# A recurrence on one core: inputs of both batch halves in one instruction, the state in unused ends of buffers, and a sixth place for the layer's blocks

## The chip, the cores and the metric

The kernel runs on one core of a Trainium2 chip. The metric is the device time of one execution in microseconds (us). Three runs of the kernel before took 1663.87, 1656.67 and 1659.29 us, a median of 1659.29. A further execution, taken by the hardware profiler, gives the profile; it took 1664.5 us, of which the profile's span covers 1661.4.

The engines have these names: TensorE (PE: matrix products and transposes), VectorE (DVE), ScalarE (ACT), GpSimd (POOL) and SyncE (SP), which here issues transfers (DMA). SBUF is the on-chip memory, PSUM the memory into which TensorE writes. Shapes are given as partitions x elements.

## What is computed

The input x has 16 images of 56 x 56 positions with 128 channels. Cut to what matters:

```python
x = x + window_attention(group_norm(x))          # 7x7 windows, shifted, 4 heads
t = to_tokens(x)                                 # [16, 3136, 128]
t = t + linear_attention(layer_norm(t))          # cumulative, elu + 1
n = layer_norm(t)
Wx = batch_norm(n @ W.T)                         # over all 16 * 3136 tokens; gamma, beta
y = 0                                            # [16, 128]
for i in range(3136):
    y = sigmoid(Wx[:, i] + y @ V.T)
    t[:, i] = t[:, i] + y
return from_tokens(t)
```

The change concerns the last loop, the recurrence, and the residual that is added to it. W, V and the batch norm's factors are small and stay on the chip; x3 below is t before the recurrence, xs is n @ W.T before the batch norm.

## The kernel before

**Until 1497 us: the two attention stages.** Image by image, a planner (`Plan`) lays out the steps of windows, linear attention and projection on the engines by given costs, and the order it finds is written out. At the end of each image, x3 goes to a buffer in DRAM (`x_d` in the profile), and so does xs (`xs_d`, written from `staged`). For the last image, whose last part never leaves the chip, GpSimd copies from `staged` (L356). The batch norm's factor `bsc` and shift `bsh` come from statistics over all images (`bst` holds those of the parts); VectorE computes them at 1499 to 1502 us, L1684 to L1703, with one step on GpSimd (L1695).

**From 1497 us: the recurrence.** 3136 steps in a row would be too long. Each image's steps are cut into 32 segments (`SEG`) of 98 steps (`CH`), and all 16 x 32 segments run side by side. A segment's start is the end of the one before, which isn't known yet. So twelve steps of warm-up (`WARM`) are run ahead: the last twelve of each segment, started from nothing, give a start `y0` for the segment after it. At the end, `yend` (the true ends) is compared with `y0` (L1895 to L1907), and only where they differ is the loop repeated; with these inputs it isn't.

A step is done in two halves of the batch, `g` = 0 and 1, 8 images each, 8 x 32 = 256 columns. Steps are taken in pairs: 6 pairs of warm-up, 49 pairs of the main loop. The order is written out by hand, and the engines follow it through semaphores:

- **VectorE, `inputs` (L1773):** multiplies xs by `bsc` and writes it into a PSUM buffer `z_buf`. There are six of these, three for each half, each with a pair's two steps (128 x 512 elements, one PSUM bank). It is done two pairs ahead, between the two steps of a pair, one instruction per half. Blocks of xs hold 7 steps (`KB`); a pair whose two steps lie in two blocks needs two instructions of 256 elements per half. That happens at 7 of the 49 pairs.
- **TensorE (L1785):** adds V times the state to `z_buf`, 128 x 256 for each half-step, as two passes in the profile. **ScalarE (L1788)** takes the sigmoid with `bsh` as bias and writes the new state `y` to SBUF.
- **TensorE (L1822):** transposes the state of the step before, two transposes of 128 x 128 in each half-step, into a PSUM tile `pot` of which there are two.
- **VectorE, `plus_layer` (L1831):** after both halves adds the tile to the x3 block in place (128 x 512).
- **SyncE:** after every 7 steps the finished x3 block is stored (L1837, 1792 KB), and a later block is loaded (`load_x3`, L366, 1792 KB) into the place of the block before, which waits until that block's store has landed. xs blocks come the same way (`load_xs`, L344, 1680 KB).

There are 14 blocks of each kind. xs has a ring of five places. x3 has five too: `x3_ring` begins with three buffers that earlier stages used (`xw_buf` twice, `oT_buf`; in the profile these names), and two tiles of its own (`x_ring` in the profile). The loads that can be issued before the loop are issued at 1490 to 1499 us. Block m of x3 takes the place of block m - 5, and its load is issued behind the store of block m - 4. The last x3 block is stored in two pieces, the last one of 768 KB.

The state of four steps is kept in the pool `ryo` (two buffers of a pair each, `y` or `y_a` in the profile), y0 and yend have tiles of their own, and y0 is set to zero by GpSimd (L1721). Six matmuls of zeros (L1734) prepare the PSUM buffers once.

Of the kernel before, what the change touches and what calls it, by code (L numbers as in the profile page):

```python
# [10 lines left out]
F32 = mybir.dt.float32  # L11
AF = mybir.ActivationFunctionType
ALU = mybir.AluOpType
# [11 lines left out]
KB = 7  # L25
# [209 lines left out]
def tile_conv_attn_hybrid(  # L235
# [19 lines left out]
    nc = tc.nc  # L255
    B, H, W, C = x.shape
    P = 128
# [17 lines left out]
    NU = H // WS  # L275
# [10 lines left out]
    NQ = B // 4  # L286
# [10 lines left out]
    xw_bufs = [hold.tile([P, NU, 512], F32, name=f"xw_buf{i}") for i in range(2)]  # L297
    oT_buf0 = hold.tile([P, NU, 512], F32, name="oT_buf0")
# [59 lines left out]
    def flat(to):  # L358

        dims = " ".join("abc"[: len(to.shape) - 1])  # L360
        return to.rearrange(f"p {dims} -> p ({dims})")
# [60 lines left out]
    bst = const.tile([P, B * NS, 6], F32, name="bst")  # L422
# [7 lines left out]
    with ExitStack() as s1:  # L430
# [141 lines left out]
        s = issued = plan.step("SP", 0.1, -1.0, lambda: None, takes=[weights], lag=19.0)  # L572
# [987 lines left out]
        for b in range(B):  # L1560
# [12 lines left out]
            for g in range(NG):  # L1573
# [3 lines left out]
                up, xs, pj = token_group(  # L1577
                    b,
                    g,
                    b * NG + g,  # L1580
                    t,
                    loaded[g] if b else turns[g],
                    [rows[u] for u in need],
                    oT_buf,
                    xt_bs[g],
# [107 lines left out]
        bsc = const.tile([P, 1], F32, name="bsc")  # L1693
# [16 lines left out]
    SEG = NCH  # L1710
    GB = B // 2
# [3 lines left out]
    )  # L1715
    with ExitStack() as s2:
        rin = s2.enter_context(tc.tile_pool(name="rin", bufs=1))
        ryo = s2.enter_context(tc.tile_pool(name="ryo", bufs=2))
        y0 = rin.tile([P, B, SEG], F32, name="y0")
        yend = rin.tile([P, B, SEG], F32, name="yend")  # L1720
        nc.gpsimd.memset(y0, 0.0)  # L1721


# [1 line left out]
        psum = bass.MemoryType.PSUM  # L1725
        ps_s = s2.enter_context(tc.tile_pool(name="ps_s", bufs=1, space=psum))
        ps_o = s2.enter_context(tc.tile_pool(name="ps_o", bufs=2, space=psum))
        z_bufs = [
            ps_s.tile([P, 2, GB, SEG], F32, name=f"z_buf{i}") for i in range(6)
        ]  # L1730
        BF16 = mybir.dt.bfloat16
        zeros = y0.rearrange("p b s -> p (b s)").bitcast(BF16)[:, 0 : B * SEG]
        for i in (0, 3, 1, 4, 2, 5):
            nc.tensor.matmul(  # L1734
                z_bufs[i].rearrange("p k b s -> p (k b s)"),
                ident.bitcast(BF16)[:, 0:P],
                zeros,
                start=True,
                stop=True,
                skip_group_check=True,  # L1740
            )
# [7 lines left out]
        xs_ring += [xt for xt in xt_bufs if all(xt is not to for to in used)]  # L1749
        xs_ring += [rin.tile([P, G * NG, C], F32, name=f"xs_ring{i}") for i in range(2)]  # L1750

        x3_ring = [ahead["x3"][m] for m in range(3)]
        x3_ring += [rin.tile([P, NQ, KB, C], F32, name=f"x3_ring{i}") for i in range(2)]
        NX, N3 = len(xs_ring), len(x3_ring)

        def xs_of(m):
            to = ahead["xs"][m] if m >= NJ - 2 else xs_ring[m % NX]
            return to.rearrange("p n c -> p (n c)").rearrange(
                "p (b k n) -> p b k n", b=B, k=KB
            )  # L1760
# [5 lines left out]
        def inputs(pair):  # L1766

            j, ns, slot, _ = pair
            (m, k), (m2, k2) = divmod(j, KB), divmod(j + 1, KB)
            parts = [(m, k, 0, 2)] if m == m2 else [(m, k, 0, 1), (m2, k2, 1, 1)]  # L1770
            for g in range(2):
                for m, k, i, n in parts:
                    nc.vector.tensor_scalar(  # L1773
                        z_bufs[3 * g + slot][:, i : i + n, :, 0:ns],
                        xs_of(m)[:, GB * g : GB * (g + 1), k : k + n, 0:ns].rearrange(
                            "p b k s -> p k b s"
                        ),
                        bsc,
                        None,
                        ALU.mult,  # L1780
                    )

        def step(z, y_prev, y):
            if y_prev is not None:
# [5 lines left out]
        def segments(n, prev):  # L1790


            warm = prev is None


            pairs = []
            if warm:
                prev = [None, None]
                for j in range(CH - WARM, CH, 2):
                    pairs.append((j, SEG - 1, len(pairs) % 3, True))  # L1800
            for j in range(0, CH, 2):
                pairs.append((j, SEG, len(pairs) % 3, False))

            def load_inputs(m):
                if m not in ahead["xs"] or n != "a" and m < NJ - 2:
                    load_xs(xs_ring[m % NX], m, 0, B - 1)
                    last_xs(xs_ring[m % NX], m)

            def load_layer(m):
                first = NQ - 1 if n == "a" and m in ahead["x3"] else 0  # L1810
                load_x3(x3_ring[m % N3], m, first, NQ)

            blocks = {}

            def turned_half(at, h):

                m, k = at
                y = blocks[at]
                if h == 0:
                    blocks["po"] = ps_o.tile([P, NQ, C], F32, tag="o", name=f"pot_{n}{m}_{k}")  # L1820
                for q in range(NQ // 2 * h, NQ // 2 * (h + 1)):
                    nc.tensor.transpose(  # L1822
                        blocks["po"][:, q, :],
                        y[:, 4 * q : 4 * (q + 1), :].rearrange("p b s -> p (b s)"),
                        ident,
                    )

            def plus_layer(at):
                m, k = at
                o = x3_of(m)  # L1830
                nc.vector.tensor_tensor(  # L1831
                    o[:, :, k, :], blocks["po"], o[:, :, k, :], ALU.add
                )
                cuts = (KB // 2 + 1, KB) if m == NJ - 1 else (KB,)
                if k + 1 in cuts:
                    k0 = 0 if k + 1 == cuts[0] else cuts[0]
                    nc.sync.dma_start(  # L1837
                        out_q[:, :, KB * m + k0 : KB * m + k + 1, :], o[:, :, k0 : k + 1]
                    )

                    if k == KB - 1 and m and m - 1 + N3 < NJ:
                        load_layer(m - 1 + N3)

            for m in range(3):
                load_layer(m)
            for m in range(NX):
                load_inputs(m)
                if m >= 3:
                    load_layer(m)
            assert N3 == NX  # L1850
            inputs(pairs[0])
            inputs(pairs[1])
            last = None
            for p, (j, ns, slot, warming) in enumerate(pairs):
                y = ryo.tile([P, 2, B, SEG], F32, tag="y", name=f"y_{n}_{p}")
                if not warming:
                    for i in range(2):
                        blocks[divmod(j + i, KB)] = y[:, i]
                for i in range(2):
                    for g in range(2):  # L1860
                        gb = slice(GB * g, GB * (g + 1))
                        if not warming:
                            to = y[:, i, gb, :]
                        elif j + i == CH - 1:
                            to = y0[:, gb, 1:SEG]
                        else:
                            to = y[:, i, gb, 0:ns]
                        z = z_bufs[3 * g + slot][:, i, :, 0:ns]
                        if not warming and j + i == 0:
                            prev[g] = y0[:, gb, :]  # L1870
                        step(z, prev[g], to)
                        prev[g] = to
                        if last is not None:
                            turned_half(last, g)
                    if last is not None:
                        plus_layer(last)
                    if not warming:
                        last = divmod(j + i, KB)
                    if i == 0 and p + 2 < len(pairs):
                        inputs(pairs[p + 2])  # L1880
                        j2, _, _, warming2 = pairs[p + 2]
                        m2 = j2 // KB
                        if not warming2 and (j2 + 2) // KB > m2 and m2 + NX < NJ:
                            load_inputs(m2 + NX)
            nc.vector.tensor_copy(yend, blocks[NJ - 1, KB - 1])
            turned_half(last, 0)
            turned_half(last, 1)
            plus_layer(last)
# [2 lines left out]
            segments("a", None)  # L1891


        d = ryo.tile([P, 2, B, SEG], F32, tag="y", name="seam")[:, 0, :, 0 : SEG - 1]
        nc.vector.tensor_tensor(  # L1895
            d, yend[:, :, 0 : SEG - 1], y0[:, :, 1:SEG], ALU.subtract
        )
# [92 lines left out]
```

## Time and profile before

| | |
|---|---|
| runs | 1663.87, 1656.67, 1659.29 us; median 1659.29 |
| profiled execution | 1664.5 us |
| its span | 1661.4 us |
| instructions | 63385 |
| TensorE / VectorE / ScalarE / GpSimd busy | 1615.4 / 1398.1 / 1183.5 / 1272.0 us |
| bytes moved | 322.03 MB, mean 194 GB/s |
| first sigmoid of the warm-up, last `plus_layer` | about 1502, 1652.3 us |

All stamps are microseconds from the start of the span. A line of a timeline gives the start, the length, the engine, the kernel's line, the operation, output and inputs; "x2" says that two were drawn together, and square brackets hold the idle time before it and what ended it. "SPq" is SyncE issuing a transfer. A group's line ends in "busy us, mean ns of one | idle time before". Each z matmul of a half-step is in the profile as two passes, each transpose as one. In the slices, each digit is the busy share in tenths.

### The profile page before, as it was taken

The page shows a single profiled execution, that of the slowest core. Times are in us where ns is not written, and L with a number is a line of the kernel's source. Part 1 is how long each engine was busy: PE and PEld are TensorE (multiplying, and loading weights), DVE is VectorE, ACT ScalarE, POOL GpSimd, SP SyncE. Part 2 cuts the span into 40 slices and gives each one's busy share as a digit, 9 for nine tenths or more (in the row PEclk, how much of TensorE's full clock was granted, in tenths as well). Part 3 has the DMA queues.
Part 4 walks back from the last instruction along what each step waited for, and adds up shares of the span by engine and source line. Part 5 has one row for each costly group of instructions (what it writes and reads, how often), then busy time and mean ns, then how long its engine had stood idle before and what let it go on. Part 6 is the DMA issues. An engine that isn't in the chain of part 4 may idle for free.

```text
span 1661.4 us, 63385 instructions
## 1 busy us (share of the span) xinstructions
PE 1615.4 (97%) x25458; PEld 1308.8 (79%) x25459; DVE 1398.1 (84%) x3044; ACT 1183.5 (71%) x3156; POOL 1272.0 (77%) x2154
## 2 busy tenths in 40 slices
PE   7899999999999999999999999999999999999997
PEld 6678787887878887878888778878888887876876
DVE  5779987897989888987979798978898786757997
ACT  5577776777777777777677777767677776766765
POOL 6788978897989898888989889878889786770000
PEclk9999999999999999999999999999999999999999
DMA  5486767677677768586766777776755655558999
GB/s 137 109 186 158 192 151 172 187 167 208 154 204 166 199 153 206 149 208 169 194 165 156 204 168 196 167 191 156 196 148 155 159 160 147 190 183 342 403 419 379
DMA packets 776720, 322.03 MB, mean 194 GB/s; under 512 B 400481, under 2 KB 760161, under 8 KB 774625
## 3 DMA queue, kind: packets, MB, share of 16 engines
q1 hardware_dynamic: 774832, 317.10, 69.9%
q8 instruction: 202, 3.31, 0.9%
q10 hardware_dynamic: 1584, 0.79, 0.2%
q14 instruction: 102, 0.83, 0.2%
HBM read 171.54 MB, written 146.24 MB: 191 GB/s over the span
## 4 chain that ended last, share of the span: by engine, by line
PE 69%; POOL 8%; DVE 7%; SPq 5%; DMA 5%; issue 3%; ACT 2%; DVEq 0%; POOLq 0%; ACTq 0%
PE bank L864 8%; PE bank L1269 8%; PE bank L885 5%; PE pair L909 5%; PE state_bank L1412 4%; PE pair L964 4%; PE pair L1401 4%; PE bank L1317 4%; PE pair L1404 4%; PE bank L1502 4%; PE bank L1372 4%; PE pair L983 4%; SPq L1072 4%; PE bank L1234 4%; PE z_buf L1785 2%
## 5 line engine op out<-in xcount | busy, mean ns | idle before, releaser
L954 POOL TENSOR_TENSOR p_buf<-p_buf,rc 128x784 f32<-128x784 f32 x128 | 194.4, 1519 | 42.7 <-DVE rc L951 14.2
L1269 PE MATMUL bank<-xnT,awc_sb 128*128 128x512 f32 (+1 forms) x448 | 212.9, 557 | 3.3 <-DVE xnT L1139 2.7
L935 POOL TENSOR_TENSOR s<-s,mx 128x784 f32<-128x784 f32 x128 | 192.2, 1502 | 30.8 <-DVE mx L932 28.5
L1279 ACT ACTIVATE r<-bank,bqk_neg 128x512 f32<-128x512 f32 (+1 forms) x224 | 143.4, 640 | 76.9 <-PE bank L1269 67.3
L1412 PEld LDWEIGHTS state_bank<-v_buf,k 128*128 128x128 f32 x768 | 125.4, 191 | 52.1 <-issue 26.7
L1292 DVE SCALAR_TENSOR_TENSOR f<-bank,bqk_one,r 128x512 f32<-128x512 f32 (+1 forms) x224 | 147.5, 658 | 12.6 <-ACT r L1288 12.1
L1412 PE MATMUL state_bank<-v_buf,k 128*128 128x129 f32 x768 | 155.4, 284 | 1.3 <-ACT state L1424 1.1
L974 ACT COPY pT<-pair 128x904 f32<-128x904 f32 x128 | 118.7, 927 | 51.0 <-PE pair L964 41.3
L1401 PE MATMUL pair<-state,f 128*128 128x129 f32 x768 | 153.1, 281 | 0.6 <-issue 0.6
L1424 ACT COPY state<-state_bank 128x129 f32<-128x129 f32 x384 | 107.0, 279 | 65.5 <-PE state_bank L1412 63.9
L1401 PEld LDWEIGHTS pair<-state,f 128*128 128x128 f32 x768 | 123.4, 192 | 37.0 <-issue 21.8
L920 DVE TENSOR_TENSOR s<-pair,wmask_sb 128x784 f32<-128x784 f32 x128 | 122.7, 958 | 34.2 <-PE pair L909 30.0
L909 PEld LDWEIGHTS pair<-kT,q_buf 32*49 32x49 f32 x8192 | 106.4, 121 | 41.9 <-issue 15.7
L949 DVE TENSOR_REDUCE sm<-p_buf 128x16 f32<-128x784 f32 x128 | 121.6, 950 | 18.6 <-ACT p_buf L945 18.3
L1223 POOL TENSOR_TENSOR xt_buf<-xt_buf,bout_sb 128x512 f32<-128x512 f32 (+1 forms) x112 | 129.1, 1158 | 10.7 <-DMA xt_buf<-in_x_dram 10.5
L1788 ACT ACTIVATE y_a<-z_buf,bsh 128x256 f32<-128x256 f32 (+1 forms) x218 | 103.0, 473 | 47.4 <-PE z_buf L1785 43.3
L1288 ACT ACTIVATE r<-r 128x512 f32<-128x512 f32 (+1 forms) x224 | 131.9, 589 | 2.4
L1785 PE MATMUL z_buf<-y_a,fvT_sb 128*128 128x256 f32 (+1 forms) x432 | 131.0, 389 | 0.4 <-ACT y_a L1788 0.4
L909 PE MATMUL pair<-kT,q_buf 32*49 32x49 f32 x8192 | 122.8, 206 | 2.8 <-issue 2.4
L964 PE MATMUL pair<-ident,p_buf 113*128 113x113 f32 x1024 | 120.9, 261 | 3.1 <-POOL p_buf L954 2.8
L964 PEld LDWEIGHTS pair<-ident,p_buf 113*128 113x128 f32 x1024 | 107.5, 142 | 20.5 <-issue 11.2
L932 DVE TENSOR_REDUCE mx<-s 128x16 f32<-128x784 f32 x128 | 121.5, 949 | 0.9
(170 smaller groups left out, 4697.1 us busy)
## 6 DMA issues: line engine op xcount, KB each, us to landing
x_d<-xt_buf SPq DMA_DIRECT2D x96, 256.0 KB, 2.6
xt_buf<-in_x_dram SPq DMA_DIRECT2D x93, 256.0 KB, 3.2
spare<-in_x_dram SPq DMA_DIRECT2D x60, 392.0 KB, 4.5
xs_d<-staged SPq DMA_DIRECT2D x15, 1568.0 KB, 6.9
xna_d<-spare SPq DMA_DIRECT2D x90, 256.0 KB, 2.7
xnk_d<-f SPq DMA_DIRECT2D x90, 256.0 KB, 3.0
xnf_d<-spare SPq DMA_DIRECT2D x90, 256.0 KB, 2.8
spare<-xna_d SPq DMA_DIRECT2D x256, 64.0 KB, 2.1
```

The costliest lines, as they stand in the source:

```text
L864: nc.tensor.matmul(d[key], wqkv_sb[:, j * P : (j + 1) * P], xk, start=True, stop=True)
L909: nc.tensor.matmul(sc[64 * hh : 64 * hh + WT, hp, w * WT : (w + 1) * WT], qT[r : r + HD, w * WT : (w + 1) * WT], d["kT"][r : r + HD, w * W ...
L935: nc.gpsimd.tensor_tensor(d["sf"], d["sf"], d["mx"].unsqueeze(2).to_broadcast([P, nb, WT]), ALU.subtract,)
L954: nc.gpsimd.tensor_tensor(prf, prf, d["rc"].unsqueeze(2).to_broadcast([P, nb, WT]), ALU.mult)
L964: nc.tensor.transpose(pt[:, hp, w2, 0:NQ2], pr[0:NQ2, hp, 2 * w2 : 2 * w2 + 2, :].rearrange("p w k -> p (w k)"), ident[0:NQ2, 0:NQ2],)
L1269: nc.tensor.matmul(d[f"p{j}"], awc_sb[:, j * P : (j + 1) * P], d["xT"][:, :nt], start=True, stop=True,)
L1279: nc.scalar.activation(d[f"r{j}"], d[f"p{j}"], AF.Relu, bias=bqk_neg[:, j : j + 1], scale=-1.0,)
L1288: nc.scalar.activation(d[f"r{j}"], d[f"r{j}"], AF.Exp, scale=-1.0)
L1292: nc.vector.scalar_tensor_tensor(d[key][:, :nt], d[f"p{j}"], bqk_one[:, j : j + 1], d[f"r{j}"], ALU.add, ALU.max,)
L1401: nc.tensor.matmul(to, chunk(d["f0"], cc), t["states"][c], start=True, stop=False)
L1412: nc.tensor.matmul(t["pd"], d["k"][:, cc, :], v1[:, cc, :], start=c == 0, stop=True, skip_group_check=True,)
L1785: nc.tensor.matmul(z, fvT_sb, y_prev, start=False, stop=True, skip_group_check=True)
```

## The change

There are three parts, all within the recurrence:

1. **A pair's inputs for both halves in one instruction.** The six `z_bufs` of one bank become three of two banks, laid out image, step, segment in place of step, image, segment. `inputs` writes a plain pair with one instruction of 128 x 1024 elements; a pair that lies in two blocks with two of 128 x 512. A half-step's z, which was 256 elements in a row, is now 8 runs of 32 at a stride of 64, for TensorE and for ScalarE.
2. **State in unused ends of buffers.** y0, yend and the states of two steps (`ys`, in place of the four steps in `ryo`) lie in the last 512 elements of `xw_bufs[0]`, `xw_bufs[1]` and `oT_buf0`, and in `bst`, parts which the x3 blocks don't reach. The zeroing of y0 and the zero matmuls are the same in number.
3. **A sixth place for x3.** `x3_ring` gets a third tile of its own. One more block is loaded ahead of the loop, and block m follows the store of block m - 5.

In the order of instructions that comes out, TensorE, ScalarE, VectorE and SyncE keep the order they had before 1497 us. GpSimd's zeroing of y0 moves: it was the first thing after the last image's work and now stands within that work, between L1490 and L1119 (at 1444 us in the profile of before). In the recurrence, the first `inputs` instruction stands, as before, ahead of the second instruction of `bsh` (L1703). SyncE's order is the same but for the x3 loads, each of which comes one store earlier, the first of them behind the load of block 4.

```diff
-        ryo = s2.enter_context(tc.tile_pool(name="ryo", bufs=2))
-        y0 = rin.tile([P, B, SEG], F32, name="y0")
-        yend = rin.tile([P, B, SEG], F32, name="yend")
+        NY = B * SEG
+        def tail(to):
+            return flat(to)[:, NU * 512 - NY :].rearrange("p (b s) -> p b s", b=B)
+        y0, yend = tail(xw_bufs[0]), tail(xw_bufs[1])
+        ys = [tail(oT_buf0), flat(bst)[:, 0:NY].rearrange("p (b s) -> p b s", b=B)]
         nc.gpsimd.memset(y0, 0.0)
...
-        z_bufs = [
-            ps_s.tile([P, 2, GB, SEG], F32, name=f"z_buf{i}") for i in range(6)
-        ]
+        z_bufs = [ps_s.tile([P, B, 2, SEG], F32, name=f"z_buf{i}") for i in range(3)]
...
-        for i in (0, 3, 1, 4, 2, 5):
+        for i in (0, 1, 2, 3, 4, 5):
             nc.tensor.matmul(
-                z_bufs[i].rearrange("p k b s -> p (k b s)"),
+                z_bufs[i // 2][:, GB * (i % 2) : GB * (i % 2 + 1)].rearrange(
+                    "p b k s -> p (b k s)"
+                ),
...
-        x3_ring += [rin.tile([P, NQ, KB, C], F32, name=f"x3_ring{i}") for i in range(2)]
+        x3_ring += [rin.tile([P, NQ, KB, C], F32, name=f"x3_ring{i}") for i in range(3)]
...
-            for g in range(2):
-                for m, k, i, n in parts:
-                    nc.vector.tensor_scalar(
-                        z_bufs[3 * g + slot][:, i : i + n, :, 0:ns],
-                        xs_of(m)[:, GB * g : GB * (g + 1), k : k + n, 0:ns].rearrange(
-                            "p b k s -> p k b s"
-                        ),
-                        bsc,
-                        None,
-                        ALU.mult,
-                    )
+            for m, k, i, n in parts:
+                to = z_bufs[slot][:, :, i : i + n, 0:ns]
+                xs = xs_of(m)[:, :, k : k + n, 0:ns]
+                if n == 2 and ns == SEG:
+                    to = to.rearrange("p b k s -> p (b k s)")
+                    xs = xs.rearrange("p b k s -> p b (k s)")
+                elif n == 1:
+                    to, xs = to[:, :, 0], xs[:, :, 0]
+                nc.vector.tensor_scalar(to, xs, bsc, None, ALU.mult)
...
-            assert N3 == NX
+            for m in range(NX, N3):
+                load_layer(m)
...
-                y = ryo.tile([P, 2, B, SEG], F32, tag="y", name=f"y_{n}_{p}")
                 if not warming:
                     for i in range(2):
-                        blocks[divmod(j + i, KB)] = y[:, i]
+                        blocks[divmod(j + i, KB)] = ys[i]
...
-                            to = y[:, i, gb, :]
+                            to = ys[i][:, gb, :]
...
-                            to = y[:, i, gb, 0:ns]
-                        z = z_bufs[3 * g + slot][:, i, :, 0:ns]
+                            to = ys[i][:, gb, 0:ns]
+                        z = z_bufs[slot][:, gb, i, 0:ns]
```

More of the change, by code (lines that the diff above doesn't have):

```diff
@@ L1750, in tile_conv_attn_hybrid @@
         xs_ring += [rin.tile([P, G * NG, C], F32, name=f"xs_ring{i}") for i in range(2)]
+        assert all(len(to.shape) == 3 for to in (*xw_bufs, oT_buf0, bst))
         x3_ring = [ahead["x3"][m] for m in range(3)]
-        x3_ring += [rin.tile([P, NQ, KB, C], F32, name=f"x3_ring{i}") for i in range(2)]
+        x3_ring += [rin.tile([P, NQ, KB, C], F32, name=f"x3_ring{i}") for i in range(3)]
         NX, N3 = len(xs_ring), len(x3_ring)
@@ L1891, in tile_conv_attn_hybrid @@
             segments("a", None)
-        d = ryo.tile([P, 2, B, SEG], F32, tag="y", name="seam")[:, 0, :, 0 : SEG - 1]
+        d = ys[0][:, :, 0 : SEG - 1]
         nc.vector.tensor_tensor(
```

## The prediction

> **What bounds the kernel now.** I read the slices of the page first, to see where the changed part (the recurrence, from about 1501 us on) differs from the rest. The last four of the 40 slices, 1495 to 1661 us, hold it:
>
> ```profile
> PE   7899999999999999999999999999999999999997
> DMA  5486767677677768586766777776755655558999
> GB/s 137 109 186 158 192 151 172 187 167 208 154 204 166 199 153 206 149 208 169 194 165 156 204 168 196 167 191 156 196 148 155 159 160 147 190 183 342 403 419 379
> ```
>
> TensorE is full nearly everywhere, but DMA is full only in these slices, at about 400 GB/s. So in the stage that changes there are two candidates. The windows separate them (columns: window, length, then busy time and count of each engine, clock, DMA share, GB/s):
>
> ```profile
> 1516.00:1520.00 4.00, 3.96 (x21) 2.82 (x21) 2.10 (x3) 2.90 (x7) 0.00 (x0) 1.00 0.56 225
> 1520.00:1524.00 4.00, 3.85 (x25) 3.02 (x24) 3.64 (x8) 2.84 (x6) 0.37 (x1) 1.00 0.28 56
> 1552.00:1600.00 48.00, 47.32 (x288) 39.24 (x287) 47.38 (x78) 33.80 (x72) 1.12 (x3) 1.00 1.02 418
> 1600.00:1652.00 52.00, 49.09 (x288) 40.31 (x287) 46.36 (x76) 33.88 (x72) 0.00 (x0) 0.97 1.02 418
> 1652.00:1656.00 4.00, 0.19 (x2) 0.11 (x2) 2.82 (x6) 0.00 (x0) 0.00 (x0) 0.83 1.04 405
> ```
>
> From 1552 us on TensorE, VectorE and DMA are all full. The last window decides: TensorE is through at 1652, and DMA still moves 405 GB/s. The DMA slices of 1640 to 1661.4 (40 slices of 0.535 us) show the drain:
>
> ```profile
> GB/s 415 422 429 415 422 429 424 409 422 415 415 402 422 422 422 422 422 422 422 415 433 395 394 390 406 414 412 398 406 411 375 335 242 147 78 11 0 15 31 15
> ```
>
> The traffic runs out in slice 36, at 1659.25; the span ends 2.1 us later. The end is therefore set by bytes, not by steps. The bytes had a gap earlier: before the first result block can be stored, nothing is left to load. SyncE's issues and the DMA slices of 1497 to 1525 (0.7 us each) show it:
>
> ```profile
> 1498.68 0.44 SPq L366 DMA_DIRECT2D x_ring<-x_d  x1
> 1522.31 0.32 SPq L344 DMA_DIRECT2D spare<-xs_d  x1
> 1528.51 0.39 SPq L1837 DMA_DIRECT2D out_dram<-xw_buf  x1
> ...
> 1537.52 0.46 SPq L366 DMA_DIRECT2D xw_buf<-x_d  x1
> ```
>
> ```profile
> GB/s 435 422 365 422 434 365 461 422 442 442 384 356 431 410 415 410 415 476 515 404 422 461 422 319 426 399 410 425 420 405 95 15 0 0 0 0 0 261 154 288
> ```
>
> No load is issued for 24 us, and from 1518 to 1522.3 almost nothing moves.
>
> **The sixth place.** It lets block 5 of the layer be issued right behind block 4, at about 1499, not behind the second store at 1537.52. The block is 1792 KB = 1.835 MB, at 418 GB/s 4.39 us, which is the length of the gap. Every later block is issued one store earlier; the number of bytes is the same. On SyncE the issue takes 0.44 us, with nothing behind it until 1522.31. So 4.4 us of a queue that drains without a pause until the end go into a time when it was empty. Term: **-4.4 us**, on the path. Bounds: 0, if the hole only moves to about 1530 (between the two stores DMA is not full either), and -4.4, the whole block.
>
> **Does the compute allow it?** TensorE's half-steps stand 0.652 us apart in the loop (196 of them, 127.9 us). Its z matmuls run from 1517.38 to 1649.85, 5.3 us more than 195 pitches. I went through the starts for what exceeds the pitch: 2.5 us at six block crossings (0.37 to 0.45 each), 2.3 us at one wait for a layer block, 0.4 us just after it:
>
> ```profile
> 1616.20 0.44 PE L1822 MATMUL pot_a<-ident,y_a 128*128 128x128 f32 x2 [2.07 <-DVE xw_buf L1831]
> ```
>
> ```profile
> 1615.45 1.29 DVE L1831 TENSOR_TENSOR xw_buf<-pot_a,xw_buf 128x512 f32<-128x512 f32 x2 [2.32 <-DMA xw_buf<-x_d]
> ```
>
> The first is TensorE waiting for VectorE, the second VectorE waiting for the block. With every block a store earlier this wait (2.3 + 0.4) should go.
>
> **One input instruction per pair.** Rows of 1550 to 1600 us (the groups by shape):
>
> ```profile
> L1831 DVE TENSOR_TENSOR x_ring<-pot_a,x_ring 128x512 f32<-128x512 f32 x16 | 10.8, 684 | 0.1
> L1773 DVE TENSOR_SCALAR z_buf<-xs_ring,bsc 128x512 f32<-128x512 f32 x14 | 9.8, 744 | 0.0
> L1773 DVE TENSOR_SCALAR z_buf<-xs_ring,bsc 128x256 f32<-128x256 f32 x6 | 2.8, 480 | 0.1
> ```
>
> Back to back on VectorE the starts stand 0.653 us apart for 512 elements, 0.395 for 256 and 0.60 for plus_layer. That is 1.008 ns an element and 0.137 us per instruction. A plain pair costs 2 x 0.60 + 2 x 0.653 = 2.51 us of TensorE's 4 x 0.652 = 2.61. It then costs 1.20 + 0.137 + 1.032 = 2.37. A crossing pair costs 3.10 us now (four instructions took 1.90 at 1576.90 to 1578.80) and so holds TensorE up; with two of 512 elements it costs 1.20 + 2 x 0.653 + up to 0.19 (the second part waits for the first) = 2.70, 0.09 over the pair's time against 0.24 of slack in each neighbour. So the 2.5 us at crossings go. VectorE's saving of 0.14 in a plain pair lies behind TensorE: nothing.
>
> The first input instruction stands ahead of the second half of bsh, which the first sigmoid needs. 128x496 elements take 0.73 us now; twice as many at 1.008 ns add 0.50: the warm-up starts **+0.5 us** later. This lies on the compute path only, with DMA full until 1518; without the drain as cover it would cost its 0.5.
>
> Compute end: 1652.32 (last plus_layer) - 2.5 - 2.7 + 0.5 = 1647.6. The last store, 768 KB, then needs 0.786 MB / 0.418 = 1.9 us and, like the 64 KB loads of the page, 2.1 us to land: 1651.6 at the earliest. DMA's end is 1659.25 - 4.4 = 1654.9 and still the later one, by 3.3 us. So the compute savings, 5.2 us, are priced at nothing: the drain covers them. By themselves they would be nothing, too.
>
> **State in buffer tails.** y goes from four steps' buffers to two. The sigmoid that overwrites step t stands behind the z matmul of t+2 anyway, and TensorE runs the transposes of t ahead of that matmul: no new wait, 0. The first y0 use waits for transfers long landed: 0. The six matmuls of zeros into z change their order only: 0.
>
> **The y0 memset** leaves a place where GpSimd idles:
>
> ```profile
> 1497.02 0.53 POOL L1721 MEMSET y<- 128x512 f32 x1 [1.86 <-PE bank L1502]
> ```
>
> It now stands among GpSimd's work of the last image, between L1490 at 1444.11 and L1119 at 1445.34. Behind it are L954's p_buf (1448.51), for which TensorE's L964 waits, and an idle time of 3.02 us before 1453.04. Bounds 0 (absorbed there) and +0.53 (all on the path, which moves everything after it); I take +0.3, the middle, as L954 is waited for. Where it stood, the copies behind it at 1497.70 wait for ScalarE's staged at 1497.56 anyway: nothing is won.
>
> **z in PSUM.** A half-step's z becomes 8 runs of 32 at a stride of 64, for TensorE's write and for ScalarE's read; before it was 256 in a row. No such stride is in the trace. The nearest rows are the warm-up's 8 runs of 31 at a stride of 32, with the contiguous ones of the same stretch and of the loop:
>
> ```profile
> L1785 PE MATMUL z_buf<-y_a,fvT_sb 128*128 128x248 f32 x44 | 13.7, 425 | 0.4 <-ACT y_a L1788 0.4
> L1785 PE MATMUL z_buf<-y,fvT_sb 128*128 128x256 f32 x4 | 1.2, 431 | 0.0
> L1785 PE MATMUL z_buf<-y_a,fvT_sb 128*128 128x256 f32 x150 | 45.0, 380 | 0.0
> ```
>
> Broken rows took 425, contiguous ones beside them 431, so the difference to 380 comes with the stretch, not with the breaks. ScalarE's rows are 467 broken and 473 whole. I take 0; the bounds are 0 and 45 ns a pass (the first against the third row).
>
> [...]
>
> **Sum.** -4.4 + 0.3 = -4.1 us. The profiled execution took 1664.5 us (span 1661.4 and 3.1 around it) and should take 1660.4, with a span of 1657.3. The three runs' median is 1659.29, 5.2 below that execution; the difference applied to it gives **1655.2**.
>
> **Rivals.**
> 1. *Broken rows in PSUM cost (slower).* Place: every z matmul of the loop, two passes a half-step, 392 in all. Price at 45 ns: 17.6 us, with the matmul at the head of TensorE's full queue. Compute end 1647.6 + 17.6 = 1665.2, landing 4.0 later, span 1671.3: +9.9, so 1669. It decides from 3.3 us on (8 ns a pass), and makes the kernel slower than before from 3.3 + 4.4 = 7.7 us on (20 ns). For: TensorE has no slack at all. Against: 425 beside 431.
> 2. *The hole only moves.* The block is in early, but then 1522 to 1550 is emptier, as the stores come no sooner; the drain ends where it did. For: DMA moves 225 and 56 GB/s around the gap and is not full until about 1550. Against: each later block follows a store earlier and fills it. Time: 0 to -1, about 1659.
> 3. *The compute sets the end.* More of DMA's lost time is won than one block. Then the landing is 1651.6 at the earliest, the span 1653.7: -7.7, 1651.6; without the 0.5 us of the first input, 1651.1.
>
> **How the numbers follow.** The forecast has 0.60, rival 1 0.09, rival 2 0.13, rival 3 0.18. The three runs spread from 1656.67 to 1663.87, so a median can lie 2 us off by itself. The low end is rival 3's 1651.1 less 1.5; the high end rival 2's 1659 with this spread; rival 1 is left out. 0.5% is 8.3 us, about what a measurement of this kernel can tell from no change. Faster by more than that, below 1651.0, is half of rival 3, which lies at that edge (0.09), and a tenth of the forecast (0.06): 0.15. Rival 1 is slower, 0.09. The rest, 0.76, is within it.
>
> **What would show it.** Right: in 1518 to 1522 DMA at about 400 GB/s, no issue at 1537.52 from L366 but one at 1499; the last traffic near 1655; no 2 us wait of VectorE for a layer block; one 128x1024 input row of about 1.25 us per pair; no excess at crossings; z matmul rows at 380 to 385. Wrong: z matmul rows above 400 or half-steps over 0.66 us apart (rival 1); a new low stretch in 1525 to 1550 and the drain again to 1659 (rival 2); the last landing within 4.2 us of the last plus_layer (rival 3).

## The result

The changed kernel takes 1767.99 us, the median of six runs (1762.54 to 1773.19), against 1660.92 (1656.67 to 1664.28, six runs) of the kernel before: 1.064 times as long (95% interval 1.0617 to 1.0662). The forecast was 1655.2, and even the high end of its range, rival 2's 1659 with the spread of the runs, lies more than 100 us below. The profiled execution has a span of 1767.0 us, 105.6 more than before.

The slices of the page show two things that were not there before: TensorE is no longer full in the last stage, and for one slice the granted clock is halved.

```profile
PE   8899999999999999999999999999999999777775
PEclk9999999999999999999999999999999999599999
```

Where the time went, from the starts of the first and last z matmul (L1785, now L1789) and of the first transpose (L1822, now L1826) in the two traces:

| stretch | before | after | difference |
|---|---|---|---|
| start to first z matmul | 1502.4 | 1499.9 | -2.5 |
| warm-up, to the first transpose | 15.5 | 37.3 | +21.7 |
| main loop, to the last z matmul | 132.1 | 218.4 | +86.3 |
| the rest | 11.3 | 11.4 | +0.1 |

**The main loop.** The timeline of TensorE and ScalarE, one pair of steps (start, length, what, idle time before and what ended it):

```profile
1590.45 0.47 ACT L1792 ACTIVATE oT_buf<-z_buf,bsh 128x256 f32<-128x256 f32 x1 [0.23 <-PE z_buf L1789]
...
1591.71 0.47 ACT L1792 ACTIVATE oT_buf<-z_buf,bsh 128x256 f32<-128x256 f32 x1 [0.79 <-PE z_buf L1789]
...
1592.24 0.70 PE L1789 MATMUL z_buf<-oT_buf,fvT_sb 128*128 128x256 f32 x2 [0.34 <-ACT oT_buf L1792]
...
1593.50 0.70 PE L1789 MATMUL z_buf<-oT_buf,fvT_sb 128*128 128x256 f32 x2 [0.35 <-ACT bst L1792]
...
1594.26 0.60 PE L1789 MATMUL z_buf<-bst,fvT_sb 128*128 128x256 f32 x2
```

The z matmul at 1592.24 opens a new step on the first half of the batch and waits for the sigmoid at 1591.71, which is the *other* half's: a value that it doesn't read. The one that it does read comes from the sigmoid at 1590.45 and has been there since 1590.92. Of four z matmuls in a pair three wait so, and the starts stand 1.21, 1.26, 1.26 and 0.75 us apart, 4.49 a pair in place of 2.61. Only the first one in a new z tile (1594.26) goes ahead freely. Counted by the starts of half-steps, the table's stretch holds 48 pairs. At 1.88 us more for each this is 90.4; 6.4 us of stalls that the kernel before has in it now have room, and 1.7 us come from the half clock, which lasts into the first pairs: 85.7, close to the table's 86.3, which goes from the first transpose.

**The warm-up.** Windows (columns as above: busy and count of PE, PEld, DVE, ACT, POOL; clock, DMA share, GB/s):

```profile
1500.00:1520.00 20.00, 14.24 (x28) 7.08 (x29) 5.17 (x6) 6.08 (x13) 0.00 (x0) 0.53 0.97 401
1520.00:1540.00 20.00, 15.21 (x32) 8.15 (x31) 4.27 (x4) 6.11 (x13) 0.00 (x0) 0.50 0.00 1
1560.00:1580.00 20.00, 14.98 (x72) 9.87 (x69) 12.08 (x15) 8.54 (x18) 0.38 (x1) 1.00 0.68 255
```

The same waits, and on top of them half the clock, from 1501 to about 1542 us. DMA, idle from 1520 to 1540 us and busy for a share of 0.68 in the main loop's window, is no longer full, and none of the longest waits of the main loop is for a transfer.

**What came as forecast.** The groups of 1550 to 1600 us, and SyncE's issue of two x3 blocks, the second of them the sixth place:

```profile
L1789 PE MATMUL z_buf<-bst,fvT_sb 128*128 128x256 f32 x45 | 14.7, 407 | 4.7 <-ACT oT_buf L1792 4.7
L1785 DVE TENSOR_SCALAR z_buf<-xs_ring,bsc 128x1024 f32<-128x1024 f32 x5 | 6.4, 1278 | 0.0
```

```profile
1495.46 5.68 SPq L366 DMA_DIRECT2D x_ring<-x_d  x2
```

One input instruction of 1.28 us a pair, the sixth block early, and DMA full until 1518. None of it is on the path now. The mean of 407 for a z matmul is not its own pace; see the first experiment.

### The profile page after: what moved, and what is told of

It is laid out like the page before. It is cut to its first block, busy times and chain, and to the rows that moved or that the text cites. A ratio compares the mean times of both kernels' runs of the same rounds, so it can differ in the third digit from the quotient of the medians.

```text
span 1767.0 us, 63245 instructions
## 1 busy us (share of the span) xinstructions
PE 1663.2 (94%) x25459; PEld 1318.1 (75%) x25459; DVE 1394.8 (79%) x2981; ACT 1184.4 (67%) x3156; POOL 1274.1 (72%) x2154
## 4 chain that ended last, share of the span: by engine, by line
PE 72%; POOL 9%; ACT 6%; DVE 4%; SPq 4%; issue 3%; DMA 2%; ACTq 0%; DVEq 0%; POOLq 0%
PE z_buf L1789 9%; PE bank L1269 8%; PE bank L864 7%; PE bank L885 5%; PE pair L909 5%; PE pair L964 4%; PE state_bank L1412 4%; PE pair L1401 4%; PE bank L1317 4%; PE bank L1372 4%; PE pair L983 4%; PE pair L1404 4%; PE bank L1502 4%; PE bank L1234 4%; ACT oT_buf L1792 3%
## 5 line engine op out<-in xcount | busy, mean ns | idle before, releaser
L964 PEld LDWEIGHTS pair<-ident,p_buf 113*128 113x128 f32 x1024 | 107.6, 142 | 21.7 <-issue 11.6
L1789 PE MATMUL z_buf<-oT_buf,fvT_sb 128*128 128x256 f32 (+1 forms) x220 | 83.2, 462 | 41.3 <-ACT oT_buf L1792 21.2
L945 ACT ACTIVATE p_buf<-s 128x784 f32<-128x784 f32 x128 | 113.0, 883 | 10.9 <-POOL s L935 10.3
```

What stands on the lines that cost most here:

```text
L964: nc.tensor.transpose(pt[:, hp, w2, 0:NQ2], pr[0:NQ2, hp, 2 * w2 : 2 * w2 + 2, :].rearrange("p w k -> p (w k)"), ident[0:NQ2, 0:NQ2],)
L1789: nc.tensor.matmul(z, fvT_sb, y_prev, start=False, stop=True, skip_group_check=True)
```

## The experiments

Theory A: the wait is the price. A z tile that both halves share ties each z matmul to the sigmoid before it, and the half clock follows from the idle TensorE. Rivals: the broken rows of z in PSUM; the state in two steps' buffers; a low clock of its own cause.

**One z tile per half.** The changed kernel but for

```diff
-        z_bufs = [ps_s.tile([P, B, 2, SEG], F32, ...) for i in range(3)]
+        z_bufs = [ps_s.tile([P, GB, 2, SEG], F32, ...) for i in range(6)]
...
-            for m, k, i, n in parts:
-                to = z_bufs[slot][:, :, i : i + n, 0:ns]
+            for g in range(2):
+                for m, k, i, n in parts:
+                    to = z_bufs[3 * g + slot][:, :, i : i + n, 0:ns]
```

> The changed kernel with one z tile of one bank for each half again (six in place of three), and so one input instruction per half; z in broken runs, state in buffer ends and the sixth place stay. Theory (the shared tile makes each z matmul wait for the other half's sigmoid, and the idle TensorE then loses its clock): both go; half-steps 0.652 us apart, clock 1.0 in the warm-up, about 1655 us. Rival (broken runs of 32 in PSUM slow the matmul or the sigmoid): half-steps stay well over 0.652; at 45 ns a pass about 1669 us, and if the stride were the whole cause, near the changed kernel's 1768.

Measured: 1659.05 us, 0.9966 of the kernel before on the same chip (0.9944 to 0.9987). The changed kernel stood at 1.064, so the whole loss is gone, and about a third of a per cent is gained. Half-steps stand 0.65 us apart, the clock is 1.00. The group of 1501 us to the end, and two windows:

```profile
L1788 PE MATMUL z_buf<-oT_buf,fvT_sb 128*128 128x256 f32 x196 | 58.6, 381 | 0.0
```

```profile
1516.00:1520.00 4.00, 4.00 (x24) 3.20 (x23) 1.90 (x4) 2.96 (x7) 0.00 (x0) 1.00 1.02 414
1520.00:1524.00 4.00, 3.84 (x25) 2.97 (x23) 3.93 (x8) 2.55 (x7) 0.37 (x1) 1.00 0.92 309
```

The rows are as broken as in the changed kernel, 8 runs of 32 at a stride of 64, and a pass takes 381 ns, beside 380 whole. So the stride costs nothing here, and the 407 above is a mean that takes in passes that waited: in the next experiment, with the same waits and whole rows, it is 423. The windows show the gap of before filled: 414 and 309 GB/s where there were 225 and 56.

**The shared tile alone.** The kernel before but for

```diff
-        z_bufs = [
-            ps_s.tile([P, 2, GB, SEG], F32, name=f"z_buf{i}") for i in range(6)
-        ]
+        z_both = [ps_s.tile([P, 2, 2, GB, SEG], F32, ...) for i in range(3)]
+        z_bufs = [z_both[i % 3][:, i // 3] for i in range(6)]
```

> The kernel before with one thing changed: the two halves' z buffers of a pair lie in one tile of two banks. z in whole rows of 256, one input instruction per half, five places, and the state's buffers as before. Theory (shared tile): three of four z matmuls of a pair wait for the sigmoid of the half-step before; a pair takes 4.48 us in place of 2.61, 49 times 1.87 = 92 us more, the warm-up some 20 more with its clock at 0.5, less the 5 of the stalls that have room now: about 1765 us. Rival (the stride or the state in two steps' buffers is the cause): no change, 1657 to 1664.

Measured: 1769.5 us, 1.0613 (1.0577 to 1.0649). TensorE's timeline:

```profile
1593.35 0.70 PE L1784 MATMUL z_buf<-y_a,fvT_sb 128*128 128x256 f32 x2 [0.35 <-ACT y_a L1787]
...
1594.11 0.60 PE L1784 MATMUL z_buf<-y_a,fvT_sb 128*128 128x256 f32 x2
```

The pattern is the same, with nothing changed but which tile the halves' z lie in. Rows are whole, states and places as before, one input instruction per half, and each half keeps its own 128 x 512 elements (a bank in the kernel's layout) in both. This one line is nearly the whole result.

**The clock.** The changed kernel, with two products that nobody reads behind each z matmul of the warm-up:

```diff
                         step(z, prev[g], to)
+                        if warming and prev[g] is not None:
+                            stir(stirred, 2)
```

> The changed kernel with two more 128x128 products of the identity, which nobody reads, behind each z matmul of the warm-up. Theory (the clock of 0.5 from 1501 to about 1543 us comes from the TensorE that the wait leaves idle): the clock stays at 1.0; a warm-up pair takes 4.5 to 4.8 us in place of 6.14, 8 to 10 us less in all, about 1759 us. Rival (the low clock has another cause, such as the pause before the first z matmul): clock still 0.5, and the added products make the warm-up longer, 1768 us or more.

Measured: 1759.92 us, 1.0544 (1.0511 to 1.0577). The window of the warm-up:

```profile
1500.00:1520.00 20.00, 17.03 (x103) 14.04 (x103) 10.24 (x18) 8.31 (x19) 2.81 (x8) 1.00 1.00 412
```

The clock stays at 1.00, with TensorE busy for 3.60 to 3.77 of every 4 us from 1506 to 1518 us, and the warm-up takes 28.5 us, not 37.3, with more work in it. So the low clock follows from the idle TensorE, and in the warm-up it costs at least 8.8 us on top of the waits.

**The sixth place alone.** The kernel before with the third part of the change, and the second that it needs for room:

```diff
-        x3_ring += [rin.tile([P, NQ, KB, C], F32, ...) for i in range(2)]
+        x3_ring += [rin.tile([P, NQ, KB, C], F32, ...) for i in range(3)]
```

> The kernel before with the sixth place for the layer's blocks and the state in unused ends of buffers; inputs and z tiles as before. Theory (the drain of the transfers sets the end): the gap of 1518 to 1522 us is filled, the last traffic ends 4.4 us sooner, about 1655 us; the wait of 2.3 us for a layer block goes. Rival (the hole only moves): 1659 to 1661, DMA not full between 1525 and 1550.

Measured: 1662.1 us, 0.997 (0.9952 to 0.9988): the same, within the intervals, as with a tile per half. The last store lands 152.4 us behind the first z matmul, in place of 156.9, and the wait for a layer block is gone: the z matmuls run over 144.1 us, not 147.7.

**All but the sixth place.** The kernel of the first experiment with `range(2)` for the x3 tiles.

> The kernel with one z tile per half of the last series (broken runs, state in buffer ends), with five places for the layer's blocks as before the change. Theory (the sixth place alone carries the gain of about 0.35% that was measured with it): the gap of 1518 to 1522 us and the wait of 2.3 us for a layer block are back, and the time is that of the kernel before, 0.998 to 1.002 of it. Rival (the state's place or the layout brings it): 0.996 to 0.997 again.

Measured: 1665.61 us, 1.0007 (0.9991 to 1.0024). The last store lands 156.6 us behind the first z matmul, as before (156.9). In these two kernels the sixth place brings the whole gain.

**Sharing without the wait.** The changed kernel, where the second half of the batch runs one pair behind the first, so that their z matmuls alternate between two tiles; with it come places for four steps' states, and inputs one pair ahead in place of two:

```diff
+            for u in range(total + 2):
+                if u % 2 == 0 and u // 2 + 1 < len(pairs):
+                    inputs(pairs[u // 2 + 1])
...
+                for g in range(2):
+                    if 0 <= u - 2 * g < total:
+                        half(u - 2 * g, g)
```

> The changed kernel, shared z tiles, merged inputs and all, but the second half of the batch runs one pair behind the first, so that two successive z matmuls never write the same tile; states of four steps, inputs one pair ahead in place of two. Theory (the wait comes only from successive half-steps in one tile): half-steps 0.652 us apart in the main loop, no excess at the block crossings, clock 1.0; two half-empty steps at the start and two at the end cost about what the crossings (2.5 us) gave; about 0.996 of the kernel before, as with a tile per half. Rival (sharing a tile costs whatever the order): pairs of 4.5 us, about 1.06.

Measured: 1662.3 us, 0.998 (0.9966 to 0.9994). TensorE's and VectorE's timelines:

```profile
1590.62 0.60 PE L1790 MATMUL z_buf<-ys,fvT_sb 128*128 128x256 f32 x2
...
1591.28 0.60 PE L1790 MATMUL z_buf<-xw_buf,fvT_sb 128*128 128x256 f32 x2
```

```profile
1575.06 0.75 DVE L1786 TENSOR_SCALAR z_buf<-spare,bsc 128x512 f32<-128x512 f32 x1
1575.90 0.75 DVE L1786 TENSOR_SCALAR z_buf<-xt_buf,bsc 128x512 f32<-128x512 f32 x1
1576.56 1.28 DVE L1836 TENSOR_TENSOR xw_buf<-pot_a,xw_buf 128x512 f32<-128x512 f32 x2
1577.76 1.28 DVE L1786 TENSOR_SCALAR z_buf<-xt_buf,bsc 128x1024 f32<-128x1024 f32 x1
```

The tiles are shared, the inputs are merged, and no z matmul waits for the other half. It is the order of the half-steps within a tile that decides. The crossing at 1575.06 takes 1.50 us on VectorE, and TensorE shows nothing of it. What that gives (0.37 to 0.45 us at a crossing) goes into the half-empty steps at both ends: the two starts behind the first z matmul stand 1.24 apart each. It is no faster than the first experiment: the z matmuls run over 143.9 us (144.1 there), but the last store lands 154.5 us behind the first z matmul (152.2 there), for which no run has the cause.

**What sets the end.** The prediction said: bytes. In the changed kernel the last store's traffic is over by about 1761 us, 6 us ahead of the end, and yet the span ends 9.2 us behind the last plus_layer, as it did before (9.1). So I took bytes away: the kernel before without the store of block 9 (`if m != 9:` ahead of it).

> The kernel before without the store of block 9 (its part of the output is not written); its loads stay. One look, read from the first z matmul of the warm-up: before, the last plus_layer ended 150.0 us after it, the last traffic 156.9 and the span 159.0. Theory (the drain of bytes sets the end): the traffic ends up to 4.4 us sooner, but not sooner than 4.0 us behind the last plus_layer: 154.0, the span 156.1. Rival (the end hangs on the last steps): 156.9 and 159.0 again.

In this one execution the last store lands 154.7 us behind the first z matmul, 2.2 sooner, and the span ends at 159.2 (before: 159.0). The bytes alone do not set the end. The events at the branch behind the seam check (L1911 before, L1912 in this kernel), in ns, and when they start:

```profile
L1911 SPq EVENT_SEMAPHORE  x8: 17/17/17, 1659.3 to 1659.8; - x8
...
L1911 PEldq COMPARE_BRANCH  x1: 3699/3699/3699, 1656.1 to 1656.1; - x1
...
L1911 DVEq EVENT_SEMAPHORE  x1: 21/21/21, 1660.4 to 1660.4; - x1
```

```profile
L1912 SPq EVENT_SEMAPHORE  x8: 17/17/17, 1665.8 to 1666.3; - x8
...
L1912 DVEq EVENT_SEMAPHORE  x1: 21/21/21, 1669.3 to 1669.3; - x1
```

SyncE passes when the last store has landed (1659.3); TensorE's branch takes 3.7 us, and VectorE is heard of again at 1660.4. In the second kernel SyncE is ready 3.5 us ahead of VectorE. So two ways lead to the end: the last landing, and the last step with the seam check and the branch. Two more runs, of one execution each, are without the branch and its loop (`n_bad` and the `tc.If` are left out):

> The kernel before without the branch at the end (the comparison of yend with y0 is still computed, the loop that would be repeated where they differ is left out of the program). One look, from the first z matmul of the warm-up; in the profile of before the last plus_layer ended at 149.95, the last store landed at 156.9, VectorE came out of its branch at 158.0, the span ended at 159.0. Theory (two ends that lie almost together, the last landing and the way through the branch): the landing is still at 156.9 and now sets the end, 158.4 to 159.0. Rival (the branch alone sets the end): the span ends 2 to 3 us sooner, 156 to 157.

The store lands at 156.8, the span ends at 157.7, 1.3 sooner: less than the rival's 2 to 3, but a little more than expected, as the way from the landing to the end is 0.9 us here, in place of 2.1.

> The same without the branch, and without the store of block 9 as in the run before this series. Theory (two ends close together): now both are sooner; with the landing at 154.7, as in the run with the store left out, the span ends at about 156.8. Rival (something else behind the last steps sets the end): 159 again.

The store lands at 153.8, the span ends at 154.6, 4.4 sooner, and 2.2 sooner than expected: the landing came 0.9 ahead of 154.7, and the way from it to the end is 0.8. Taken away alone, the bytes give nothing and the branch 1.3; together they give 4.4. The two ends lay about one microsecond apart.

## Why the prediction was wrong

**The step that failed** is "One input instruction per pair". It priced the instructions and not the buffer that they need. Merging the halves' inputs puts both halves' z into one tile, and with that comes a wait that the sum does not have: 86.3 us in the main loop and 21.7 in the warm-up, the half clock that follows from it included. The part "State in buffer tails" asked which new waits there are, "z in PSUM" what the new layout costs a pass; nothing asked who else now writes and reads the z tile. No rival had it: the slower one was about the stride, which costs nothing (381 against 380 ns).

The price stood in the trace of before:

```profile
1561.74 0.60 PE L1785 MATMUL z_buf<-y_a,fvT_sb 128*128 128x256 f32 x2
...
1562.38 0.47 ACT L1788 ACTIVATE y_a<-z_buf,bsh 128x256 f32<-128x256 f32 x1 [0.18 <-PE z_buf L1785]
...
1563.05 0.60 PE L1785 MATMUL z_buf<-y_a,fvT_sb 128*128 128x256 f32 x2
```

There a half-step goes from its z matmul (1561.74) over its sigmoid (1562.38 to 1562.85) to the same half's next z matmul (1563.05): 1.31 us, in which TensorE does the other half. A wait between the halves takes away just this overlap. Three of four half-steps at some 1.26 us and one at 0.75 are what came.

**"The end is therefore set by bytes, not by steps"** failed too. Only half of it held: the last landing was one of two ends, and not the later one. The last traffic at 1659.25 and the span's end 2.1 us later fitted the story, but VectorE's event at 1660.4 lay between them. With the sixth place the landing moves by 4.5 to 4.7 us (156.9 to 152.4 and 152.2; the term said 4.4) and the steps by 3.6 (147.7 to 144.1), so both ends move. The span from the first z matmul falls from 159.0 to 155.2 with a tile per half and to 156.6 with the sixth place alone. The forecast of -4.1 us was therefore near what the sixth place gives (0.9966 and 0.997, 5 to 6 us), partly for the wrong reason: the compute savings, priced at nothing, were needed for it. What the steps win there is the wait for the layer block; the crossings keep their 2.5 us in both kernels, and only the merged inputs of the lagged kernel take those away.

**"5.3 us more than 195 pitches"** was misread as well. It counts from 1517.38, where the main loop's third half-step starts. The first starts at 1516.11, and all 196 take 6.6 us more than their pitches. The missing 1.3 lie behind the wait for the layer block:

```profile
1613.53 0.60 PE L1785 MATMUL z_buf<-y_a,fvT_sb 128*128 128x256 f32 x2
...
1617.15 1.06 PE L1785 MATMUL z_buf<-y_a,fvT_sb 128*128 128x256 f32 x2
1618.00 0.63 PE L1822 MATMUL pot_a<-ident,y_a 128*128 128x128 f32 x2
1618.43 1.06 PE L1785 MATMUL z_buf<-y_a,fvT_sb 128*128 128x256 f32 x2
```

The granted clock is 0.5 from 1617.1 to 1620.5, and with it a z matmul takes 1.06 us in place of 0.60. So the clock fell behind a wait (TensorE idle for 2.07 us until 1616.20) in the kernel before already. The wait and its low clock cost some 4.0 us, not 2.7: from the z matmul at 1613.53 to that at 1620.76 it is 7.23 us, where five pitches are 3.26. The steps gain 3.6 where the sixth place takes the wait away.

**What held:** the gap of 1518 to 1522 us and its filling; the wait for a layer block, which lasted 1.8 to 2.7 us in the profiles of the kernel before and the four others with its pace and five places (their z matmuls ran over 145.9 to 148.0 us, the longer times where the clock fell behind the wait); the crossing's 1.50 us on VectorE, and 1.18 between the starts at 1577.76 and 1578.94 for 1024 elements (1.17 forecast); the first sigmoid's 0.5 us (the first input takes 1.25 in place of 0.73); the state in buffer ends, without a wait.

**Open:** the memset's 0.3 us. The first z matmul starts between 1499.9 and 1511.1 us in the traces of these kernels, and 0.3 can't be seen in that. Why the wait is set, the runs don't show: they show that it comes with the tile, with whole rows as with broken ones and although each half has its own 128 x 512 elements (a bank in the kernel's layout), and goes with separate tiles or another order. Two halves in the same bank were not run.

## What to carry to other kernels

Before two instructions are merged into one, list for the buffer that they then share everyone who writes and reads it, in order, and ask for each neighbouring pair whether one now waits for the other; a chain hidden by alternating between two halves is priced at its full length (here 1.3 us a half-step against 0.65) as soon as that answer is yes. What sets the end is found by taking it away: a queue that is full until the end may have a second end right behind it.

## What the runs showed of the hardware

**The granted clock and single waits.** Behind the wait for a layer block the clock fell to 0.5 in three of five profiles (waits of 2.2, 2.3 and 2.7 us) and stayed at 1.0 in two (1.8 and 2.0 us). Each time it came back after 3.4 to 3.5 us, in which TensorE was full; in the profile of before it was 0.5 from 1617.1 to 1620.5 us, with TensorE busy for 2.00 of 2 us from 1618.

**The granted clock and many short waits.** Two windows of the kernel with the shared tile alone, then three of the changed kernel (the second number is TensorE's busy time, the third from the end the clock):

```profile
1510.00:1514.00 4.00, 2.48 (x8) 1.27 (x8) 1.44 (x2) 1.66 (x5) 0.00 (x0) 1.00 1.07 447
1522.00:1530.00 8.00, 5.66 (x11) 2.73 (x11) 2.19 (x3) 2.34 (x5) 0.00 (x0) 0.50 0.00 0
```

```profile
1502.00:1506.00 4.00, 2.82 (x7) 1.25 (x5) 1.25 (x1) 1.40 (x3) 0.00 (x0) 0.50 1.02 416
...
1538.00:1540.00 2.00, 2.00 (x6) 1.62 (x7) 0.41 (x1) 0.47 (x1) 0.00 (x0) 0.50 0.00 0
1540.00:1542.00 2.00, 1.80 (x5) 0.96 (x4) 0.28 (x1) 0.47 (x1) 0.00 (x0) 0.50 0.01 4
```

With the shared tile alone, TensorE was busy for some 60% of the time at full clock (2.39 to 2.48 of 4 us from 1506 to 1518 us), and the clock fell at about 1520 us, 14 us into the same waits; in the changed kernel it fell at 1501. At half the clock the matmuls take longer (in the changed kernel the z matmul at 1541.03 takes 1.22 us, the one at 1542.81, with the clock back, 0.70) and the share is some 70% (2.82 of 4 us), yet the clock stayed low for 41 us: steady work at that share did not bring it back here. It came back at about 1542, when transposes had joined the matmuls and 3.80 of 4 us were busy. In the main loop it was 1.0 with TensorE busy for 76% (15.2 of 20 us). Shares at different clocks are not to be compared: 15.21 of 20 us stand in the warm-up, too, at a clock of 0.50. What sets the moment at which the clock falls or comes back, the runs don't show.

**The branch.** The compare-and-branch past the loop, which isn't repeated, held TensorE for 3.4 to 5.1 us at the end of these kernels (3.7 in the profile of before, 3.4 without the store of block 9), and VectorE's next event came 4.8 to 6.5 us behind the compared value (5.1 before, 4.9 without that store).
